# Products of the identity in TensorE's planned idle stretches, and conditioning products of 128 columns, in a two-block transformer kernel

## The chip, the cores and the metric

The kernel runs on one NeuronCore of a Trainium2 chip. The metric is the device time of one execution in microseconds (us); three runs of the kernel before gave 1361.81, 1362.93 and 1365.57. The engines are called PE (TensorE), DVE (VectorE), ACT (ScalarE), POOL (GpSimd) and SP (SyncE, which here only issues DMAs). Each executes its instructions in the order written, and waits on semaphores for the others.

## What is computed

The reference applies two transformer blocks to `x` of 16 x 256 x 256 (batch, length, channels), all in float32. The first block, conditioned on one vector per batch element, has three residual steps. The second, `L1`, is one cross attention whose norms are conditioned on other tensors.

```python
m = silu(mod) @ w_ada + b_ada                 # nine pieces of 256: shift, scale, gate x 3
h = _ln(x) * (1 + sc_msa) + sh_msa
x = x + _self_attn(h, ...) * g_msa            # 16 heads of 16, windows of 128, rolled by 64
h = _ln(x) * (1 + sc_mca) + sh_mca
x = x + _topk_cross_attn(h, context, ...) * g_mca   # softmax over the 16 largest of 256 scores
h = _ln(x) * (1 + sc_mlp) + sh_mlp
x = x + (silu(h @ w_a + b_a) * (h @ w_b + b_b) @ w_m2 + b_m2) * g_mlp    # hidden size 1024
...
ss = silu(c) @ W_ss + b_ss                    # L1: scale and shift of each norm
x = x + softmax(q k' / 4) v @ Wp + bp         # q from x, k and v from the context
```

## The kernel before

One function, `pixart_two_blocks`, treats the 16 batch elements one after another; the 256 positions of one lie as two tiles of 128 partitions. Every step is recorded with `op(...)` into a `Plan`: its engine, an estimated cost, the buffers it reads and writes, and a function that emits it. Each step also has a due time from a table (`DUE`, in thousandths of one batch element), found earlier and written into the file. `Plan.order` sorts all steps by due time; then it walks through them once with the estimated costs (`LAG`, `SWITCH`, and for DMAs `ISSUE`, `BEGIN`, `LAND`, `RATE`, `OPEN`) and keeps the time at which each engine is free. The walk does not change the order. What it decides is which of the free buffers of a kind a step takes: the one free first. `Plan.run` then emits the steps in that order, so that it is the order of every engine's queue. The kind `W` is the eight PSUM banks of 128 x 512; a bank goes back when its last reader's estimated end has passed.

The stages that the prediction speaks of, with their lines in the kernel before:

- **Conditioning** (`conditioned`, `ada_columns`, `gate_rows`). `condT` holds silu of the 16 vectors, turned to 128 channels x 2 x 16. `ada_columns` multiplies a 256 x 256 piece of a weight with it: four products (L703) with a 128 x 128 piece of the weight stationary and 16 columns of `condT` moving. DVE adds the bias (L709, L711). There are ten such pieces: six for the three norms of the first block and four for `L1`. `gate_rows` has `condT` stationary (L744); its rows go to DRAM and are loaded back for every batch element (`gate`, L377).
- **Self attention**: norm (DVE statistics L425 and L427, POOL L432 to L437 for `xn`), transposes against the identity (L449), shift and scale on ACT (L463), products with the weights (L475, and L511 for the values), scores (L780), their maxima on DVE (`maxima`, L588), which `lower` turns (L598) and sends with sixteen small DMAs into spare rows of the queries (L605), scores again the other way round (L788), exponentials (L612, ACT), the product with the values (L581), division (L538, L540 on DVE, `on` L541 on POOL), `oT` (L548), and the projection (L558), whose weights POOL has multiplied by the gate (`gw`, L404); ACT copies it out (L398) and POOL adds it to `x` (L399). `add_row` (L384) adds the gate's bias row to `x`.
- **Top-k attention**: scores (L827), then on DVE twice the eight largest (L846, L866) and their removal (L854, L871); exponentials on ACT (L859); POOL multiplies (`prT`, L875); transposes (L525), copies (L528), and L581.
- **Feed forward** (L888, L915) and the **last attention** (L932, L944).

From the second batch element on, these are interleaved: top-k of one element beside self attention of the next and feed forward and last attention of the one before. At the start there is only the first element, beside the loading of weights and the conditioning; at the end only the last one, which is treated in two halves.

```python
if o.eng == "PE" and o.mode != mode:
    t, mode = t + SWITCH[o.mode], o.mode
for p in o.after:
    t = max(t, p.end + (p.own if p.eng == o.eng else LAG.get(p.eng, 0.0)))
```

Of the kernel before, what the change touches and what calls it, by code (L numbers as in the profile page):

```python
# [163 lines left out]
SWITCH = {128: 0.18, 32: 0.2, 33: 0.12}  # L164
OWN = {"PE": 0.0, "DVE": 0.13, "ACT": 0.1, "POOL": 0.05}
LAG = {"PE": 0.22, "DVE": 0.14, "ACT": 0.18, "POOL": 0.1}
ISSUE, BEGIN, LAND, RATE, OPEN = 0.47, 0.9, 1.0, 320.0, 8


class Buf:  # L170
# [8 lines left out]


class Op:
    __slots__ = ("tag", "eng", "cost", "hold", "own", "kb", "emit", "due", "mode", "takes", "uses", "after", "start", "end", "n")


class Plan:
# [9 lines left out]
    def op(self, eng, cost, emit, r=(), w=(), also=(), mode=None, after=(), hold=None, own=None, kb=()):  # L195


        o = Op()
        o.hold, o.own, o.kb = cost if hold is None else hold, OWN.get(eng, 0.0) if own is None else own, kb
        o.eng, o.cost, o.emit, o.mode, o.n = eng, cost, emit, mode, len(self.ops)  # L200
        o.tag = self.tag
        o.after, o.takes, o.uses = {*after}, [], []
        for how, items in (("r", r), ("w", w), ("a", also)):
            for item in items:
                buf, key = item if isinstance(item, tuple) else (item, None)
                if buf.kind is not None and o not in buf.users:
                    buf.users.append(o)
                    o.uses.append(buf)
                if how == "a":
                    continue  # L210
                same = [k for k in {*buf.writers, *buf.readers} if key is None or k is None or k == key]
                for k in same:
                    if k in buf.writers:
                        o.after.add(buf.writers[k])
                    if how == "w":
                        o.after.update(buf.readers.get(k, ()))
        for how, items in (("r", r), ("w", w)):
            for item in items:
                buf, key = item if isinstance(item, tuple) else (item, None)
                if how == "r":  # L220
                    buf.readers.setdefault(key, []).append(o)
                else:
                    if key is None:
                        buf.writers, buf.readers = {}, {}
                    buf.writers[key] = o
                    buf.readers[key] = []
        o.after.discard(o)
        self.ops.append(o)
        return o

    def order(self):

        for o in self.ops:
            o.due = max([o.due, *(p.due for p in o.after)])
        done = sorted(self.ops, key=lambda o: (o.due, o.n))
        free, open_users, ends = {e: 0.0 for e in ("PE", "DVE", "ACT", "POOL", "SP")}, {}, {}  # L240
        slots = {k: [(0.0, n) for n in range(len(v))] for k, v in self.tiles.items()}
        mode, lanes, moved = None, [0.0] * OPEN, 0.0
        for o in done:
            t = free[o.eng]
# [4 lines that stand above are left out]
            for b in o.uses:  # L249
                if b.slot is None:  # L250
                    if not slots[b.kind]:
                        raise RuntimeError(f"no {b.kind} is free for {o.tag}, due {o.due}")
                    at, b.slot = slots[b.kind].pop(0)
                    t = max(t, at)
                    o.takes.append(b)
                    open_users[b], ends[b] = len(b.users), 0.0
            for b in o.uses:
                t = max([t, *(end for e, end in b.seen.items() if e != o.eng)])
            o.start = t
            for kb in o.kb:  # L260
                t = max(t, lanes.pop(0)) + ISSUE
                moved = max(t + BEGIN, moved) + kb / RATE
                lanes.append(moved + LAND)
            free[o.eng], o.end = (t, lanes[-1]) if o.kb else (t + o.hold, t + o.cost)
            for b in o.uses:
                if b.kind == "W":
                    b.seen[o.eng] = o.end + LAG[o.eng]
                ends[b] = max(ends[b], o.end + LAG.get(o.eng, 0.0))
                open_users[b] -= 1
                if not open_users[b]:  # L270
                    insort(slots[b.kind], (ends[b], b.slot))
        self.span = max(free.values())
        return done

    def run(self):
        for o in self.order():
            for b in o.takes:
                b.t = self.tiles[b.kind][b.slot]
            o.emit()


# [2 lines left out]
def pixart_two_blocks(ctx: ExitStack, tc: tile.TileContext, i: dict, out: bass.AP):  # L284
# [50 lines left out]
    for t in tiles["v"]:  # L335
        nc.gpsimd.memset(t[:, :, :, DH:NW], 1.0)
    plan = Plan(tiles)
    op = plan.op

    def rolled(ap, b):  # L340
# [288 lines left out]
        "L1_xcond_Wq", "L1_xcond_Wkv", "L1_xcond_Wp")}  # L629
    w_qkv, w_so, w_q, w_kv, w_co, w_m1, w_m2, w1_q, w1_kv, w1_p = weights.values()  # L630
    ada = {(how, g): fixed(f"ada_{how}_{g}", [P, NCC, B]) for how in ("shift", "scale") for g in (0, 1, 2, "q", "kv")}
    condT = fixed("condT", [P, NCC, B])

    last_row = fixed("last_row", [P, C])
    gates = [Buf(None, dram.tile([B, 2, C], F32, name=f"gates_{g}")) for g in range(3)]
# [37 lines left out]
    def conditioned():  # L673

        y, sy, w = Buf("h"), Buf("h"), Buf("W")
        op("SP", 0.0, lambda: nc.sync.dma_start(y.t[:B, :], i["cond_1024"]), w=[y], kb=(16,))
        op("ACT", 0.4, lambda: nc.scalar.activation(sy.t[:B, :], y.t[:B, :], AF.Tanh, scale=0.5), r=[y], w=[sy])

        def silu():
            nc.vector.scalar_tensor_tensor(sy.t[:B, :], sy.t[:B, :], 1.0, y.t[:B, :], ALU.add, ALU.mult)  # L680
            nc.vector.tensor_scalar(sy.t[:B, :], sy.t[:B, :], 0.5, None, ALU.mult)
        op("DVE", 0.8, silu, r=[y, sy], w=[sy])

        def emit():
            for c in range(NCC):
                nc.tensor.transpose(w.t[:, ts(c, B)], sy.t[:B, ts(c, P)], ident[:B, :B])
        op("PE", 0.3, emit, r=[sy], w=[w], mode=128)
        op("DVE", 0.2, lambda: nc.vector.tensor_copy(condT.t.rearrange("p c b -> p (c b)"), w.t[:, :NCC * B]), r=[w], w=[condT])

    def ada_piece(src):  # L690

# [4 lines left out]
    def ada_columns(dst, src, bias, chunk, plus_one):  # L696

        w, pm = ada_piece(src), Buf("W")

        def emit():  # L700
            for m in range(NCC):
                for c in range(NCC):
                    nc.tensor.matmul(pm.t[:, ts(m, B)], w.t[:, c, ts(m, P)], condT.t[:, c, :], start=c == 0, stop=c == NCC - 1)  # L703
        op("PE", 1.7, emit, r=[w, condT], w=[pm], mode=128)

        def out_of_it():
            for m in range(NCC):
                if plus_one:
                    nc.vector.tensor_scalar(dst.t[:, m, :], pm.t[:, ts(m, B)], col(bias, chunk + m), 1.0, ALU.add, ALU.add)  # L709
                else:  # L710
                    nc.vector.tensor_scalar(dst.t[:, m, :], pm.t[:, ts(m, B)], col(bias, chunk + m), None, ALU.add)  # L711
        op("DVE", 0.32, out_of_it, r=[pm, cols(bias)], w=[dst])


# [13 lines left out]
    def gate_rows(g, proj, value=None):  # L728

        rows = Buf("gate")  # L730
        off = (3 * g + 2) * C

        def emit():
            nc.sync.dma_start(rows.t[:B, 0, :], i["L0_xcond_b_ada"][off:off + C].partition_broadcast(B))
            nc.sync.dma_start(rows.t[:B, 1, :], i[proj].partition_broadcast(B))
        op("SP", 0.0, emit, w=[rows], kb=(16, 16))
        w, pg = ada_piece(i["L0_xcond_w_ada"][:, off:off + C]), Buf("W")
        if value:
            pv = value_bias(*value)
            op("DVE", 0.34, lambda: nc.vector.tensor_tensor(rows.t[:B, 1, :], pv.t[:B, :C], rows.t[:B, 1, :], ALU.add), r=[pv, rows], w=[rows])  # L740

        def product():
            for c in range(NCC):
                nc.tensor.matmul(pg.t[:B, :C], condT.t[:, c, :], w.t[:, c, :], start=c == 0, stop=c == NCC - 1)  # L744
        op("PE", 0.86, product, r=[w, condT], w=[pg], mode=128)

        def both():
            nc.vector.tensor_tensor(rows.t[:B, 0, :], pg.t[:B, :C], rows.t[:B, 0, :], ALU.add)
            nc.vector.tensor_tensor(rows.t[:B, 1, :], rows.t[:B, 0, :], rows.t[:B, 1, :], ALU.mult)
        op("DVE", 0.75, both, r=[pg, rows], w=[rows])  # L750
        op("SP", 0.0, lambda: nc.sync.dma_start(gates[g].t, rows.t[:B]), r=[rows], w=[gates[g]], kb=(32,))
# [344 lines left out]
```

## Time and profile before

| what | value |
|---|---|
| median of three runs | 1362.93 us (1361.81 to 1365.57) |
| the profiled execution | 1365.2 us |
| its span, first to last instruction | 1363.1 us |
| mean granted TensorE clock | 0.981 |
| PE busy | 1327.1 us, 97% of the span |
| DVE busy | 1216.9 us, 89% |
| ACT, POOL busy | 1014.4 us, 1026.4 us |
| chain that ended last | PE 87%, DVE 5% |

Times in the profile count from the start of the span. A row of the timeline gives start, duration, engine, line, operation, output and inputs, the size of the part of TensorE in use, the shapes and the number of merged instructions; in square brackets stands how long the engine had been idle before, and what ended that. A product in float32 appears as two records, a transpose as one. The granted clock is a record of its own, as a share of the full one.

### The profile page before, as it was taken

What the parts mean: (1) busy time and instruction counts of PE and PEld (TensorE: products, weight loads), DVE (VectorE), ACT (ScalarE), POOL (GpSimd) and SP (SyncE); (2) the same over time, 40 slices, a digit from 0 to 9 for tenths busy, and PEclk for the clock granted to TensorE, in tenths of its full rate; (3) what the DMA queues carried; (4) which work ended last, traced back from release to release, by engine and by line L of the source; (5) the groups of instructions that cost most, each with busy time, mean ns of one, the idle gap of its engine ahead of it and who ended that gap; (6) DMA issues with size and microseconds to landing.
All of it is one profiled execution on the core that took longest, in us unless ns stands there. A gap on an engine that the chain in (4) does not pass through costs nothing.

```text
span 1363.1 us, 38514 instructions
## 1 busy us (share of the span) xinstructions
PE 1327.1 (97%) x13464; PEld 1040.8 (76%) x13464; DVE 1216.9 (89%) x4357; ACT 1014.4 (74%) x2359; POOL 1026.4 (75%) x1552
## 2 busy tenths in 40 slices
PE   8699999999999999999999999999999999999996
PEld 6466787878778787877878787787878777787875
DVE  3699999999999999999999999999999999998734
ACT  4256778877777878777787878778787877877773
POOL 2456887878788787878878787787878787878752
PEclk9788999999999999999999999999999999999998
DMA  5412000101000010100001010001101000000000
GB/s 158 147 53 58 18 25 18 40 18 41 16 20 25 19 40 18 41 17 18 25 22 37 17 41 18 18 25 22 36 18 41 25 18 25 26 2 10 10 2 18
DMA packets 64161, 42.44 MB, mean 31 GB/s; under 512 B 37764, under 2 KB 56752, under 8 KB 63712
## 3 DMA queue, kind: packets, MB, share of 16 engines
q1 hardware_dynamic: 63967, 39.99, 10.9%
q8 instruction: 107, 1.75, 0.5%
q14 instruction: 87, 0.70, 0.2%
HBM read 35.14 MB, written 4.29 MB: 29 GB/s over the span
## 4 chain that ended last, share of the span: by engine, by line
PE 87%; DVE 5%; POOL 2%; DMA 2%; SPq 1%; issue 1%; ACT 1%; ACTq 0%; POOLq 0%; DVEq 0%
PE W L888 17%; PE W L475 11%; PE W L581 11%; PE W L525 8%; PE W L915 7%; PE W L511 6%; PE W L558 6%; PE W L944 5%; PE W L932 5%; PE W L827 5%; PE W L449 3%; PE W L788 3%; PE W L780 2%; DVE rest L854 1%; DVE rest L871 1%
## 5 line engine op out<-in xcount | busy, mean ns | idle before, releaser
L875 POOL TENSOR_TENSOR prT<-rest,prT 128x512 f32<-128x512 f32 x256 | 325.7, 1273 | 63.5 <-DVE rest L871 49.8
L859 ACT ACTIVATE prT<-W,ntop 128x256 f32<-128x256 f32 x512 | 216.8, 510 | 76.0 <-POOL ntop L848 64.3
L588 DVE TENSOR_REDUCE nm<-W 128x2 f32<-128x512 f32 (+1 forms) x384 | 236.9, 681 | 28.1 <-PE W L932 16.0
L888 PE MATMUL W<-xT,w_L_xcond_w_m 128*128 128x256 f32 (+1 forms) x1088 | 249.0, 375 | 1.5 <-ACT xT L463 1.5
L612 ACT ACTIVATE pTO<-W 128x512 f32<-128x512 f32 (+1 forms) x392 | 200.5, 613 | 62.0 <-PE W L944 37.6
L888 PEld LDWEIGHTS W<-xT,w_L_xcond_w_m 128*128 128x128 f32 x1088 | 189.1, 190 | 57.0 <-ACT pTO L612 10.9
L854 DVE MATCH_REPLACE8 rest<-top,W 128x256 f32<-128x256 f32 x512 | 208.2, 416 | 0.2 <-issue 0.2
L871 DVE MATCH_REPLACE8 rest<-top,rest 128x256 f32<-128x256 f32 x512 | 205.5, 409 | 0.0
L846 DVE MAX8 top<-W 128x8 f32<-128x256 f32 x512 | 187.0, 417 | 14.7 <-PE W L827 14.5
L866 DVE MAX8 top<-rest 128x8 f32<-128x256 f32 x512 | 187.3, 410 | 0.0
L525 PE MATMUL W<-ident,prT 128*128 128x128 f32 x1024 | 144.4, 279 | 11.1 <-POOL prT L875 11.1
L528 ACT ACTIVATE pTT<-W 128x512 f32<-128x512 f32 x256 | 148.4, 621 | 8.8 <-PE W L525 8.7
L541 POOL TENSOR_TENSOR on<-tr,rec 128x128 f32<-128x128 f32 (+1 forms) x162 | 71.0, 443 | 98.6 <-DVE rec L540 98.2
L525 PEld LDWEIGHTS W<-ident,prT 128*128 128x128 f32 x1024 | 120.3, 143 | 32.6 <-POOL prT L875 14.6
L905 POOL TENSOR_TENSOR mb<-ma,mb 128x256 f32<-128x256 f32 (+1 forms) x136 | 94.7, 697 | 62.7 <-ACT mb L903 50.6
L538 DVE STREAM_TRANSPOSE tr<-W 128x256 f32<-128x256 f32 (+1 forms) x162 | 79.2, 490 | 48.1 <-PE W L581 40.1
L915 PE MATMUL W<-w_L_xcond_w_m,h 128*128 128x256 f32 x512 | 113.8, 380 | 0.0
L581 PE MATMUL W<-pTO,v 128*32 128x128 f32 (+1 forms) x2112 | 108.1, 329 | 2.3 <-ACT pTO L612 2.0
L915 PEld LDWEIGHTS W<-w_L_xcond_w_m,h 128*128 128x128 f32 x512 | 95.9, 190 | 13.6 <-POOL prT L875 0.8
L908 POOL TENSOR_TENSOR h<-h,mb 128x256 f32<-128x256 f32 (+1 forms) x136 | 94.8, 697 | 8.3
L581 PEld LDWEIGHTS W<-pTO,v 128*32 128x32 f32 x2112 | 57.8, 111 | 42.6 <-ACT h L907 10.2
L903 ACT ACTIVATE mb<-W,half 128x256 f32<-128x256 f32 (+1 forms) x136 | 69.6, 513 | 9.7 <-PE W L888 8.4
(126 smaller groups left out, 2675.2 us busy)
## 6 DMA issues: line engine op xcount, KB each, us to landing
gate<-gates SPq DMA_DIRECT2D x48, 256.0 KB
q<-nmT SPq DMA_DIRECT2D x480, 1.0 KB
cx<-in_ctx_dram SPq DMA_DIRECT2D x19, 256.0 KB
cx<-in_ctx_dram SPq DMA_DIRECT2D x104, 32.0 KB
rest<-in_L_xcond_w_ada_dram SPq DMA_DIRECT2D x9, 256.0 KB
x<-in_x_dram SPq DMA_DIRECT2D x16, 128.0 KB
x<-in_x_dram SPq DMA_DIRECT2D x32, 64.0 KB
w_L_xcond_w_m<-in_L_xcond_w_m_dram SPq DMA_DIRECT2D x1, 2048.0 KB
```

The lines of the kernel that those rows point to most:

```text
L525: nc.tensor.transpose(w.t[:, ts(n, P)], flat[:, ts(n, P)], ident)
L581: nc.tensor.matmul(po.t[ds(NW * j, NW), ds(q0, nq)], v.t[:, kt, 8 * m + 2 * j + a, :], pT.t.rearrange("p n q -> p (n q)")[:, ds(part, nq)] ...
L588: op("DVE", 0.61, lambda j=j, s=s: nc.vector.tensor_reduce(nm.t[:, k, ds(j, groups, step=4)], s.t.rearrange("p (g k) -> p g k", g=groups), ...
L612: op("ACT", 0.24 + q * 0.0005, lambda s=s, pT=pT: nc.scalar.activation(pT.t.rearrange("p n q -> p (n q)")[:, :q], s.t[:, :q], AF.Exp), r=[ ...
L846: nc.vector.max(top.t[:, a, 0:8], s.t[:, ts(a, L)])
L854: nc.vector.match_replace(rest.t[:, a, :], top.t[:, a, 0:8], s.t[:, ts(a, L)], TAKEN)
L859: nc.scalar.activation(pr.t[:, a, :], s.t[:, ts(a, L)], AF.Exp, bias=ntop.t[:, a:a + 1])
L866: nc.vector.max(top.t[:, a, 8:16], rest.t[:, a, :])
L871: nc.vector.match_replace(rest.t[:, a, :], top.t[:, a, 8:16], rest.t[:, a, :], TAKEN)
L875: op("POOL", 1.25, lambda: nc.gpsimd.tensor_tensor(pr.t, rest.t, pr.t, ALU.mult), r=[rest, pr], w=[pr])
L888: nc.tensor.matmul(w.t[:, :q], w_m1.t[:, c, ds(n0, P)], xT.t[:, c, :q], start=c == 0, stop=c == NCC - 1)
L915: nc.tensor.matmul(pp.t[:, ts(k, C)], hs[f].t[:, ts(k, P)], w_m2.t[:, f, :], start=f == 0, stop=f == NHC - 1)
```

## The change

Three things are changed.

First, `order` marks stretches in which PE, by the estimates, sits idle for more than 1.0 us before a step. If a PSUM bank is free in time, the step gets a bank and a number `n`: as many products of an estimated 0.87 us as fit between the moment that both PE and the bank are free and 0.15 us before the step. The bank goes back to the free ones at the time of the step. `run` emits the `n` products ahead of the step: the identity times the identity repeated four times, 512 columns, into that bank. Nothing reads them.

Second, `condT` is widened from 16 to 128 columns, the rest of them zero, and `ada_columns` moves all 128; only the first 16 columns of the result are read. The product's estimated cost goes from 1.7 to 0.9. `gate_rows` still uses 16.

Third, two estimates for DMAs change: `ISSUE` from 0.47 to 0.53, and `LAND` from 1.0 to 0.4. The table of due times is the same.

```diff
-ISSUE, BEGIN, LAND, RATE, OPEN = 0.47, 0.9, 1.0, 320.0, 8
+IDLE, FILLER = 1.0, 0.87
+ISSUE, BEGIN, LAND, RATE, OPEN = 0.53, 0.9, 0.4, 320.0, 8
...
             o.start = t
+            if o.eng == "PE" and t - free["PE"] > IDLE and free["PE"]:
+                ok = slots["W"][:1]
+                n = int((t - max(free["PE"], ok[0][0]) - 0.15) / FILLER) if ok else 0
+                if n > 0:
+                    slot = slots["W"].pop(0)[1]
+                    insort(slots["W"], (t, slot))
+                    o.fill = self.tiles["W"][slot], n
...
                 b.t = self.tiles[b.kind][b.slot]
+            if o.fill:
+                self.filler(*o.fill)
             o.emit()
...
+    def filler(t, n):
+        for _ in range(n):
+            nc.tensor.matmul(t, ident, ident.unsqueeze(1).to_broadcast([P, 4, P]), start=True, stop=True)
+    plan.filler = filler
...
-    condT = fixed("condT", [P, NCC, B])
+    condT = fixed("condT", [P, NCC, P])
+    nc.vector.memset(condT.t, 0.0)
...
-                    nc.tensor.matmul(pm.t[:, ts(m, B)], w.t[:, c, ts(m, P)], condT.t[:, c, :], start=c == 0, stop=c == NCC - 1)
-        op("PE", 1.7, emit, r=[w, condT], w=[pm], mode=128)
+                    nc.tensor.matmul(pm.t[:, ts(m, P)], w.t[:, c, ts(m, P)], condT.t[:, c, :], start=c == 0, stop=c == NCC - 1)
+        op("PE", 0.9, emit, r=[w, condT], w=[pm], mode=128)
...
-                    nc.vector.tensor_scalar(dst.t[:, m, :], pm.t[:, ts(m, B)], col(bias, chunk + m), 1.0, ALU.add, ALU.add)
+                    nc.vector.tensor_scalar(dst.t[:, m, :], pm.t[:, ds(m * P, B)], col(bias, chunk + m), 1.0, ALU.add, ALU.add)
...
-                nc.tensor.matmul(pg.t[:B, :C], condT.t[:, c, :], w.t[:, c, :], start=c == 0, stop=c == NCC - 1)
+                nc.tensor.matmul(pg.t[:B, :C], condT.t[:, c, :B], w.t[:, c, :], start=c == 0, stop=c == NCC - 1)
```

## The prediction

> **What bounds the kernel now.** I read the page first. Over most of the span TensorE (PE) is full and VectorE (DVE) nearly so; only the first tenth and the last slice differ, and there the granted clock falls.
>
> ```profile
> PE   8699999999999999999999999999999999999996
> DVE  3699999999999999999999999999999999998734
> PEclk9788999999999999999999999999999999999998
> ```
>
> The second view is the table of stretches, cut where the clock changes (columns: stretch, length, busy time and instructions of PE, weight loads, DVE, ACT, POOL; clock, DMA share, GB/s).
>
> ```profile
> 15.36:32.43 17.07, 16.71 (x166) 13.70 (x164) 7.61 (x22) 11.71 (x25) 0.00 (x0) 1.00 0.33 102
> 32.43:46.08 13.65, 13.65 (x148) 10.35 (x147) 5.03 (x19) 3.93 (x8) 4.18 (x6) 0.50 0.63 191
> 46.08:63.15 17.07, 11.71 (x85) 8.02 (x84) 12.10 (x37) 4.48 (x10) 9.94 (x15) 1.00 0.35 125
> 63.15:80.21 17.06, 11.17 (x60) 7.50 (x60) 15.81 (x65) 7.21 (x16) 8.75 (x12) 0.50 0.21 64
> 80.21:100.70 20.49, 19.06 (x245) 14.69 (x244) 18.69 (x76) 13.99 (x31) 12.13 (x17) 1.00 0.11 33
> 100.70:110.94 10.24, 8.77 (x56) 5.97 (x56) 10.24 (x43) 6.57 (x15) 8.83 (x15) 0.50 0.15 44
> 134.68:1287.00 1152.32, 1150.87 (x11760) 905.88 (x11760) 1088.51 (x3914) 905.57 (x2099) 929.21 (x1379) 1.00 0.09 24
> ```
>
> The reader is to see three things. From 134.68 to 1287 PE idles 1.5 us in 1152: it is the bound, so what the start gains or loses reaches the end unchanged. The clock is halved from 32.43, 63.15 and 100.70 on, and again twice near the end; all steps are whole multiples of 3.41 us apart. The first 15.36 us are printed as clock 1.00, but eight records of L703 take 1.89 us there as in the halved stretch, against 1.06 at 29.44: they are slow too.
>
> The third view is the timeline of PE, with DVE's waits on it.
>
> ```profile
> 29.44 1.06 PE L703 MATMUL W<-condT,rest 128*128 128x16 f32 x8
> 36.20 2.09 PE L788 MATMUL W<-q,k 32*128 32x128 f32 x32
> 38.22 1.89 PE L703 MATMUL W<-condT,rest 128*128 128x16 f32 x8
> 68.24 1.11 PE L525 MATMUL W<-ident,prT 128*128 128x128 f32 x4 [8.86 <-POOL prT L875]
> 76.86 3.55 PE L511 MATMUL W<-w_L_xcond_w_kv,xT 128*128 128x256 f32 x8
> 81.94 1.17 PE L788 MATMUL W<-q,k 32*128 32x128 f32 x32
> 1317.18 1.06 PE L475 MATMUL W<-xT,w_L_xcond_Wq 128*128 128x128 f32 x8
> 1336.79 3.44 PE L932 MATMUL W<-k,q 32*128 32x256 f32 x32 [0.55 <-ACT q L497]
> ```
> ```profile
> 71.39 0.77 DVE L846 MAX8 top<-W 128x8 f32<-128x256 f32 x2 [1.08 <-PE W L827]
> 81.56 0.72 DVE L538 STREAM_TRANSPOSE tr<-W 128x512 f32<-128x512 f32 x1 [1.15 <-PE W L581]
> ```
>
> Up to about 59 us the chain of waits runs through PE, its exponentials and the small DMAs of `lower`; from 59.4 to 116 DVE is busy without a break but for those two waits on a slow PE and 0.65 us.
>
> **What the change does.** The instruction order of the changed kernel shows 26 fillers in 17 places: 18 up to about 133 us (nine places, one of them with ten, ahead of the transposes at 68.24) and 8 after 1290. SP, POOL and ACT keep their order, DVE gets one memset more, in its idle time before 2.92. PSUM banks change names, but from about 145 to 1287 every instruction waits for the same ones as before. So only start and tail move.
>
> **Prices.** A filler is one product of 512 columns, as much as four records of 256. L511's eight take 1.73 us in the chain at full clock and 3.35 at half, so a filler costs 0.87 or 1.7. Padding L703: the row at 1317.18 has its new shape (128*128, 128x128) and takes 1.06 us, what L703 takes now with 16 columns; the weight load sets it. I cost it at nothing; at half clock from 0 to +0.2 each.
>
> **Step 1, first products.** Today L475 starts at 12.09 (weights land at 11.96) and takes 5.30 us, against 3.62 at 23.99 with a full clock. The first filler stands before an L703 that idles 0.19, the second before L475, which idles 1.60. If the denser start has the clock up when L475 begins, it gains 1.7; if not, the two cold fillers (3.4 us) exceed the idle time and it ends up to 1.0 later. I take -0.7, between the ends.
>
> **Step 2, first self-attention, 31 to 59 us.** Filler three stands before L788, whose queries land at 31.39 - 0.7. PE gets there at 29.8, fills to 30.7, and the two halves of L788 end at 31.9 (now 32.25). If the clock holds: exponentials to 34.0 (2.06 as now), meanwhile L703 and filler four; L581 to 35.2; L788 at 1.17 in place of 2.09 to 36.4; L703 and filler five under the next exponentials; L581 to 39.6 (now 42.34). Here POOL comes in: it waits for the gate row (39.89 now, 39.2 then), and with `gw`, `add_row` and `on` ends at 42.3, so `oT` is there at 42.8, not 44.64. L558 then ends at 44.8 (now 48.14), and the latency chain L398, L399, statistics, `xn` keeps that shift. Filler six (behind L511, ends 50.3) is ready before `xn` (50.8). Filler seven costs 0.3 before L827, which ends at 56.45 in place of 59.42. **Top-k starts 2.95 us earlier**, of which 0.7 is step 1. What is late next is DVE: L740 needs a row that lands at 52.4 - 0.7, with its reductions it is ready at about 55.8, so there is little left behind it.
>
> **Step 3, the ten fillers.** They wait for the last L588 before L846, then need 8.7 us; the first transposed tile is 8.84 us after L846 starts. They fit with nothing to spare, and an overrun of up to 0.4 is hidden, since PE then has slack on DVE. With the clock up, L525 and L827 take 1.8 us in place of 3.2, DVE's wait of 1.08 goes, and L581 (cold L788 and L511 ahead of it) comes about 3 us earlier against DVE, so its wait of 1.15 goes too: **-2.2**. A third wait, 0.86 at 116.34 behind the stretch at 100.70, has no filler near it; I count 0, bound -0.86. The filler before L449 at 133.59 fills an idle 0.45 and 0.21 there: 0 to +0.3, taken as 0.
>
> **Step 4, tail.** Three fillers of 0.87 stand in idle times of 0.55 (L888 at 1291.13, L475 at 1334.96, L932 at 1336.79): +0.35 each, +1.05. The others fit into 0.93, 2.03 and 1.11, or run under exponentials. Against it, 32 records of L932 would take 2.3 in place of 3.44, worth 0.65 because four L588 follow; L944 and L558 behind 1346 save 1.7, of which 0.75 is left after the exponentials and a filler. Net **-0.4**, bounds -1.3 to +1.0.
>
> **Sum.** -2.95 - 2.2 - 0.4 = -5.5 us. Bounds: -8.3 with the best of steps 1, 3 and 4. The profiled execution took 1365.2 (span 1363.1), 2.3 above the median of 1362.93; so 1359.7 by its own time and 1357.4 from the median. Part of the 2.3 may be cold stretches that other executions lack, and these cannot be saved twice. I take the middle, **1358.5**.
>
> The Trainium skill (TensorE: Matmul & The Clock Gate, "What's actually happening") says that the clock is either half or full, judged in free-running windows of 3413 ns that don't start with the kernel. The trace agrees (0.50 and 1.00; 30.72 us from 32.43 to 63.15 are nine such windows). By that rule, where the cold stretches lie differs between executions.
>
> **Rivals.** *B: the fillers hold the clock less than hoped.* The first two run cold (+1.0 in place of -0.7), and after 66 us, where PE waits for DVE and nothing is filled, the clock falls again. Then top-k starts 1.25 us earlier and half of DVE's 1.08 goes, tail 0: -1.8, 1363.4 and 1361.1 by the two bases, **1362**. For it: 100.70 fell with PE 86% busy. Against it: L788 to L744 at full clock with fillers are dense.
>
> *C, slower: products of the identity do not hold the clock.* The place is the ten before the first transposes. Five run in the 5.1 us until it falls (one and a half windows), five cold: 4.4 + 8.5 = 12.9 against 8.84, +4.1, and DVE waits that much longer for L827. Fillers three to five, cold on a PE that today has no idle between 31.5 and 48, add 5.1; one and two 1.6; six and seven 0.6; the tail 1.0. Sum +12.4: **1375** (1377.6 and 1375.3, less what hides). It decides as soon as the ten start at half clock: 17 - 8.8 = 8.2 is above the whole gain. Against it: between 107.5 and 110.9, L581 and eight transposes against the same identity brought the clock back.
>
> The same page (Part 4, PE-mode transpose) says that transposes do not engage the full clock; by that rule, stretched to identity products, C would hold. The trace speaks against it at 110.94. No run here has yet shown the filler's own form.
>
> **Chances.** A measurement tells about 0.3% (4 us) from no change. Forecast 0.60: its own spread, 1354.5 to 1361, lies four parts in five below 1358.8, so 0.48 faster, 0.12 same. B 0.27: 0.02 faster, 0.25 same. C, with all that runs cold, 0.13 slower. That is 0.50, 0.37, 0.13. The range, 1354 to 1364, takes in the bounds of the sum and B; C is left out.
>
> **What would show it.** Right: no 0.50 clock between 20 and 66 us; L788 x32 in 1.17 near 35 us; the first L846 near 56.5; L525 right behind the tenth filler at 0.87 us each; DVE without the waits of 1.08 and 1.15; L449 of `xn` near 128.5 in place of 133.59; no halved window between 1336 and 1350. Wrong: fillers of 1.7 us, above all among the ten; top-k starting near 59 because the gate row or the row for L740 came last; a new fall of the clock between 66 and 100 that brings DVE's waits back.

## The result, and the profile after

The changed kernel takes a median of 1358.48 us (five runs, 1357.23 to 1358.97), the kernel before, beside it, 1362.93 (1361.81 to 1365.57). The ratio is 0.9963, 95% interval 0.9948 to 0.9977. The profiled execution took 1358.97 us with a span of 1356.9; against 1365.2 before, that is 6.2 us less, where the medians differ by 4.45. The profiled execution of before lies 2.27 above its median, that of the changed kernel 0.49. The first has a mean clock of 0.981, at the lower end of what the kernel before showed over all its runs here (0.981 to 0.991); the changed kernel had 0.994 to 0.998.

The page of the changed kernel, part 2 (the span in 40 slices, busy share and granted clock in tenths):

```profile
PE   8989999999999999999999999999999999999997
DVE  4799999999999999999999999999999999998834
PEclk9989999999999999999999999999999999999999
```

The 7 of the clock's second slice is a 9, of the two 8s behind it one is left, and the 8 of the last slice is gone; PE's second slice went from 6 to 9. The table of stretches shows the clock's falls themselves (same columns as in the prediction: length, busy time and instructions of PE, weight loads, DVE, ACT, POOL, then clock, DMA share, GB/s):

```profile
0.00:9.08 9.08, 5.09 (x17) 3.82 (x18) 4.52 (x25) 2.49 (x4) 4.72 (x16) 1.00 0.58 158
9.08:70.52 61.44, 57.33 (x494) 37.89 (x492) 36.51 (x125) 25.10 (x54) 21.19 (x33) 1.00 0.50 159
70.52:73.93 3.41, 3.20 (x15) 2.58 (x11) 3.41 (x16) 2.84 (x6) 2.73 (x3) 0.50 0.01 2
97.83:104.66 6.83, 5.96 (x47) 4.30 (x48) 6.83 (x31) 3.73 (x9) 6.40 (x10) 0.50 0.00 1
104.66:1356.00 1251.34, 1241.54 (x12697) 973.25 (x12696) 1142.33 (x4075) 965.39 (x2252) 976.78 (x1469) 1.00 0.09 24
```

Before, 47.8 us were halved (13.65, 17.07, 10.24 and twice 3.41); now 10.2 are, and none in the tail. The first row needs care: the clock is printed as 1.00 there, but its products run at half speed, as in the timeline of PE:

```profile
4.35 2.07 PE L721 MATMUL W<-condT,rest 128*128 128x128 f32 x8 [0.28 <-DVE condT L706]
7.44 1.93 PE L353 MATMUL W<-ident 128*128 128x512 f32 x2
9.20 1.05 PE L721 MATMUL W<-condT,rest 128*128 128x128 f32 x8
12.09 3.69 PE L492 MATMUL W<-xT,w_L_xcond_w_qkv 128*128 128x256 f32 x16 [0.54 <-DMA w_L_xcond_w_qkv<-in_L_xcond_w_qkv_dram]
56.15 8.85 PE L353 MATMUL W<-ident 128*128 128x512 f32 x20
1332.07 2.01 PE L950 MATMUL W<-k,q 32*128 32x256 f32 x32
```

L353 is the filler (two records each), and the lines of before that are named here are 17 or 18 further on. The first filler took 1.93, the padded L721 beside it 2.07 and then 1.05: full speed begins at 9.08 in this execution, and at 15.36 in the profiled one of before. L492 (L475 before) starts at 12.09 in both and takes 3.69 in place of 5.30. The ten fillers take 8.85, and L542 follows at 65.08 with no idle time. L950 (L932) takes 2.01 in place of 3.44.

From the first `MAX8` to 130 us, DVE's timeline has two waits on PE left:

```profile
56.24 0.76 DVE L864 MAX8 top<-W 128x8 f32<-128x256 f32 x2 [0.79 <-PE W L845]
110.74 0.76 DVE L864 MAX8 top<-W 128x8 f32<-128x256 f32 x2 [0.81 <-PE W L845]
```

The waits of 1.08 (at 71.39) and 1.15 (at 81.56) are gone. The second row is the third wait of before (0.86 at 116.34), still behind a halved stretch. The first was there before too, at the same instruction, and comes up again below:

```profile
59.40 0.76 DVE L846 MAX8 top<-W 128x8 f32<-128x256 f32 x2 [0.86 <-PE W L827]
```

It is easiest to compare kernels by three stages, each from one landmark to the next in the profiled execution: from the start to the first `MAX8` of top-k, from there to the first product of the feed forward (L888, now L906), and from there to the end of the span.

| kernel | to top-k | top-k to feed forward | to the end | profiled run, us | median, us |
|---|---|---|---|---|---|
| before | 59.40 | 76.28 | 1227.5 | 1365.2 | 1362.93 |
| changed | 56.24 | 73.86 | 1226.8 | 1358.97 | 1358.48 |
| e1 no fillers | 56.25 | 73.83 | 1227.7 | 1359.79 | 1359.79 |
| e2 16 columns | 57.07 | 74.06 | 1227.0 | 1360.12 | 1360.52 |
| e3 without ten | 56.02 | 73.82 | 1227.2 | 1359.03 | 1359.75 |
| e4 no tail | 56.07 | 73.58 | 1228.1 | 1360.17 | 1358.99 |
| f1 padding alone | 56.90 | 76.29 | 1226.7 | 1361.98 | 1360.24 |
| f2 all 16 | 59.16 | 76.40 | 1228.9 | 1366.47 | 1366.00 |
| f3 sixteen | 55.66 | 78.26 | 1226.9 | 1362.81 | 1363.03 |
| f4 one ahead of the first | 55.16 | 73.72 | 1226.0 | 1356.85 | 1357.12 |
| g1 two more at 95 | 55.55 | 74.57 | 1226.3 | 1358.44 | 1358.16 |
| g2 without the middle five | 54.60 | 74.09 | 1226.2 | 1356.94 | 1356.20 |
| h1 changed, again | 56.56 | 72.85 | 1226.8 | 1358.26 | 1359.03 |
| h2 is g2, again | 54.55 | 73.49 | 1226.3 | 1356.31 | 1356.59 |

The last column is told with intervals below. The kernel before ran beside each of the four groups of experiments (e, f, g, h), each group on another chip, with medians of 1363.30, 1362.86, 1363.43 and 1364.18.

### The profile page after: what moved, and what is told of

Read it like the earlier page. It is cut to its first block, busy times and chain, and to the rows that moved or that the text cites. A ratio compares the mean times of both kernels' runs of the same rounds, so it can differ in the third digit from the quotient of the medians.

```text
span 1356.9 us, 38607 instructions
## 1 busy us (share of the span) xinstructions
PE 1334.2 (98%) x13516; PEld 1037.8 (76%) x13516; DVE 1216.7 (90%) x4358; ACT 1015.7 (75%) x2359; POOL 1027.4 (76%) x1552
## 4 chain that ended last, share of the span: by engine, by line
PE 88%; DVE 5%; DMA 2%; ACT 2%; SPq 1%; issue 1%; POOL 1%; POOLq 0%; ACTq 0%; DVEq 0%
PE W L906 17%; PE W L492 12%; PE W L598 11%; PE W L933 8%; PE W L542 8%; PE W L528 6%; PE W L575 6%; PE W L962 5%; PE W L845 4%; PE W L950 4%; PE W L466 3%; PE W L806 2%; PE W L798 2%; DVE rest L872 1%; DVE nm L605 1%
## 5 line engine op out<-in xcount | busy, mean ns | idle before, releaser
L906 PE MATMUL W<-xT,w_L_xcond_w_m 128*128 128x256 f32 (+1 forms) x1088 | 248.7, 375 | 0.3 <-DVE nm L605 0.3
L906 PEld LDWEIGHTS W<-xT,w_L_xcond_w_m 128*128 128x128 f32 x1088 | 189.0, 190 | 56.6 <-ACT pTO L629 10.9
L542 PE MATMUL W<-ident,prT 128*128 128x128 f32 x1024 | 142.3, 276 | 3.2 <-POOL prT L893 2.6
L542 PEld LDWEIGHTS W<-ident,prT 128*128 128x128 f32 x1024 | 119.1, 142 | 24.0 <-POOL prT L893 6.2
L933 PEld LDWEIGHTS W<-w_L_xcond_w_m,h 128*128 128x128 f32 x512 | 95.9, 190 | 13.7 <-POOL prT L893 0.8
L598 PE MATMUL W<-pTO,v 128*32 128x128 f32 (+1 forms) x2112 | 105.5, 325 | 0.1
L598 PEld LDWEIGHTS W<-pTO,v 128*32 128x32 f32 x2112 | 56.3, 109 | 41.8 <-ACT h L925 9.4
```

Source lines behind the costliest of these rows:

```text
L542: nc.tensor.transpose(w.t[:, ts(n, P)], flat[:, ts(n, P)], ident)
L598: nc.tensor.matmul(po.t[ds(NW * j, NW), ds(q0, nq)], v.t[:, kt, 8 * m + 2 * j + a, :], pT.t.rearrange("p n q -> p (n q)")[:, ds(part, nq)] ...
L906: nc.tensor.matmul(w.t[:, :q], w_m1.t[:, c, ds(n0, P)], xT.t[:, c, :q], start=c == 0, stop=c == NCC - 1)
L933: nc.tensor.matmul(pp.t[:, ts(k, C)], hs[f].t[:, ts(k, P)], w_m2.t[:, f, :], start=f == 0, stop=f == NHC - 1)
```

## The experiments

The theory of the prediction is that the **fillers** keep the clock up. The rival that the trace suggests is that the **padding** does so: in the changed kernel L721 streams 128 columns through a stretch where L703 streamed 16. A third is that neither matters, and that the new DMA estimates and the other PSUM banks changed the waits. A fourth, for single groups of fillers: they cost as much as they bring.

### Fillers and padding taken apart

e1 has no fillers, but the padding and the estimates:

```diff
-                if n > 0:
+                if n > 99:
```

> The fillers are left out; the conditioning of 128 columns and the new DMA estimates stay. If the fillers hold the clock and so make the gain: back to 1362 to 1364 us, the clock halved again from about 32 us and about 63 us on, top-k's first L864 between 58 and 60 us. If the padding of the conditioning is what holds the clock: 1358 to 1360 us, full clock from about 15 to 60 us without a filler, the long idle time before the first transposes still followed by a halved clock.

Measured: 1359.79 (1358.78 to 1361.34), ratio 0.9973 (0.9961 to 0.9984). Top-k starts at 56.25, as with all fillers, but by two effects that cancel. Without the first two fillers the clock, up at 8.09, fell again from 11.50 to 14.91, L492 took 5.11, and the L721 that the changed kernel starts at 27.83 came at 29.20. What it lost there it won back behind that, where the other five fillers are missing; g2 below takes that apart. The stretch that was halved before stays at full clock:

```profile
32.43:46.08 13.65, 12.74 (x164) 8.50 (x163) 6.82 (x22) 4.23 (x9) 5.81 (x8) 1.00 0.60 179
```

e2 has the fillers, but moves 16 columns in `ada_columns`:

```diff
-                    nc.tensor.matmul(pm.t[:, ts(m, P)], w.t[:, c, ts(m, P)], condT.t[:, c, :], start=c == 0, stop=c == NCC - 1)
+                    nc.tensor.matmul(pm.t[:, ds(m * P, B)], w.t[:, c, ts(m, P)], condT.t[:, c, :B], start=c == 0, stop=c == NCC - 1)
```

> The fillers stay as they are; the conditioning products move 16 columns again. If the fillers carry the gain: 1358 to 1360 us, at most one more halved window between 30 and 45 us. If the padding matters as much: the clock halves between 30 and 46 us in spite of the fillers, top-k starts 1.5 to 3 us later than with the padding, 1360 to 1362 us.

Measured: 1360.52 (1359.37 to 1361.67), ratio 0.9980 (0.9972 to 0.9989); top-k at 57.07, clock full up to 71.73. That is the clock of its first forecast with the time of its second. Here, too, the L721 comes late, at 29.21, since full speed began at 13.71. So either part alone holds the clock from 32 to 46 us, and either alone brings half to three quarters of the whole gain (2.0 and 2.7 thousandths of 3.7). f1 is the kernel before with the padding and its lower cost estimate only; the DMA estimates are as they were (in part; ... stands for lines left out):

```diff
-    condT = fixed("condT", [P, NCC, B])
+    condT = fixed("condT", [P, NCC, P])
+    nc.vector.memset(condT.t, 0.0)
...
-                    nc.tensor.matmul(pm.t[:, ts(m, B)], w.t[:, c, ts(m, P)], condT.t[:, c, :], start=c == 0, stop=c == NCC - 1)
-        op("PE", 1.7, emit, r=[w, condT], w=[pm], mode=128)
+                    nc.tensor.matmul(pm.t[:, ts(m, P)], w.t[:, c, ts(m, P)], condT.t[:, c, :], start=c == 0, stop=c == NCC - 1)
+        op("PE", 0.9, emit, r=[w, condT], w=[pm], mode=128)
```

> The kernel before with the conditioning of 128 columns alone; no fillers, the old DMA estimates. If the padding by itself keeps the clock up through the first self attention: as without fillers, 1359.5 to 1360.5 us, no halved clock between 30 and 55 us, top-k's first L846 at 56.0 to 56.5 us. If the new estimates (other PSUM banks) had a share in that: 1361.5 to 1363.5 us.

Measured: 1360.24 (1358.21 to 1362.10), ratio 0.9979 (0.9970 to 0.9988); top-k at 56.90. Its interval and that of e1 overlap, so the DMA estimates are not needed for the gain.

f2 keeps everything of the changed kernel, also the number of fillers, their banks and waits, but fillers and `ada_columns` move only 16 columns (the edit of e2, and this):

```diff
-            nc.tensor.matmul(t, ident, ident.unsqueeze(1).to_broadcast([P, 4, P]), start=True, stop=True)
+            nc.tensor.matmul(t[:, :B], ident, ident[:, :B], start=True, stop=True)
```

> The changed kernel with conditioning products of 16 columns and fillers of 16 columns: as many products at the same places with the same weight loads, banks and waits, but hardly any columns. If the clock goes by moving columns: as before the change, 1362 to 1364.5 us, halved from about 32 to 46 us and after 60 us. If it goes by TensorE being occupied, or if waits and banks made the gain: 1358.5 to 1360.5 us.

Measured: 1366.00 (1362.24 to 1367.47), ratio 1.0019 (1.0009 to 1.0029). That is slower than the kernel before; in the profiled execution by the last stage (1228.9 against 1227.5). The stretch from 32.43 is halved again, with PE busy for all of it:

```profile
32.43:46.08 13.65, 13.65 (x151) 10.72 (x150) 5.03 (x19) 3.85 (x8) 4.16 (x6) 0.50 0.62 188
```

In its timeline of PE the scores (L806, 2.09 in place of 1.17) and L721 are back at half speed, and the short fillers run among them:

```profile
38.13 1.89 PE L721 MATMUL W<-condT,rest 128*128 128x16 f32 x8
59.08 2.40 PE L353 MATMUL W<-ident 128*128 128x16 f32 x20
```

This settles the third theory: with the same instructions, banks and waits, but few columns, the clock falls at 32.46, 63.18 and 100.73, where before had 32.43, 63.15 and 100.70. What the clock goes by is how much is streamed, not that PE has an instruction at work. The 3.41 us ahead of the fall at 32.46 show it best; here is that stretch of f2, and below it the same stage in f1, where the clock stayed up:

```profile
29.05:32.46 3.41, 3.28 (x48) 2.80 (x47) 1.45 (x10) 2.78 (x7) 0.00 (x0) 1.00 0.06 11
30.18:33.60 3.42, 3.17 (x48) 2.73 (x46) 1.26 (x9) 2.88 (x6) 0.00 (x0) 1.00 0.05 11
```

PE is busy for 3.28 us in f2 and for 3.17 in f1; what differs is above all the columns of L721 (L704 in f1). It is no accident of one profile: the mean clock over the eleven runs is 0.981 to 0.989 for f2 and 0.986 to 0.992 for f1, 0.989 to 0.991 over seven runs of e1, and 0.994 to 0.997 over twelve of e2.

### The ten and the tail

e3 leaves out only the group of ten (`n` is 10 there), e4 only the fillers of the tail (`t` is the estimated time):

```diff
-                if n > 0:
+                if 0 < n < 5:
```

> The ten fillers before the first transposes are left out; all others stay. By the prediction's step 3 they are worth 2.2 us: top-k starts near 56.3 us as with them, the clock halves near 60 us, DVE waits for L845 and L598 again (about 1.1 and 1.2 us), 1360.7 us. If DVE covers a cold PE there: 1358.5 us, no such waits.

```diff
-                if n > 0:
+                if n > 0 and t < 200:
```

> The eight fillers of the last 75 us are left out; those of the start stay. The prediction's step 4 gives them 0.4 us: 1358.9 us. The trace of the changed kernel, whose shift grew by 1.5 us in the tail, says 1360 us, with two halved windows between 1330 and 1346 us again. If they only cost time: 1357.5 us.

Measured for e3: 1359.75 (1359.03 to 1361.15), ratio 0.9971 (0.9961 to 0.9981). Without the ten the clock is halved from 58.93 to 69.17, and DVE waits for L845 a little longer than in the changed kernel (2.1 against 1.6 in all), but the stage takes 73.82 against 73.86. DVE's waits of e3 from 55 to 128 us (columns: total, times, longest):

```profile
DVE top L864 <- PE W L845: 2.1, 3, 1.1
```

And those of f1, which has no fillers either:

```profile
DVE top L847 <- PE W L828: 1.9, 2, 1.1
DVE tr L538 <- PE W L581: 1.2, 1, 1.2
```

The difference is the length of the halved stretch. In f1 it runs from 60.90 to 77.97, in f2 and before to 80.2, and all three have the wait on L581 and a stage of 76.3 or 76.4. In e1 and e3 it ends at 69.5 and 69.2, L581 (L598 there) runs at full clock, and the stage takes 73.8. So the ten are worth about 2.4 us in an execution whose cold stretch would be the long one, and nothing where it would be the short one. Which it is should go with where the 3.41 us steps lie in that execution; with one profile of each kernel that is not shown. On the medians, 0.7 to 1.3 us (1359.75 against 1358.48 and 1359.03), with overlapping intervals.

Measured for e4: 1358.99 (1357.59 to 1361.87), ratio 0.9968 (0.9955 to 0.9980), not told apart from the changed kernel. Its profiled execution has halved steps at 1330.92 and 1341.16, and the last stage takes 1228.1 in place of 1226.8, so there the tail's fillers are worth 1.3; the medians give 0 to 0.5.

### What a filler costs where it does not fit

f3 puts sixteen in place of the ten:

```diff
-                    o.fill = self.tiles["W"][slot], n
+                    o.fill = self.tiles["W"][slot], n if n < 5 else 16
```

> The changed kernel with sixteen fillers in place of the ten before the first transposes (16 columns of conditioning are not meant here; nothing else changes). Six more at 0.87 us delay L542 and L845 by 5.2 us. DVE has about 1 us to spare before it needs L845: 1358.5 + 4 = 1362 to 1363 us, and DVE waits about 4 us for L845 near 70 us. If PE catches up later all the same: 1358 to 1359.5 us.

Measured: 1363.03 (1362.32 to 1364.32), ratio 1.0003 (0.9994 to 1.0011). Timeline of PE, then DVE's waits:

```profile
55.58 14.00 PE L353 MATMUL W<-ident 128*128 128x512 f32 x32
69.42 0.60 PE L542 MATMUL W<-ident,prT 128*128 128x128 f32 x4
```
```profile
DVE top L864 <- PE W L845: 5.6, 3, 4.6
```

Sixteen at 0.87 each end 13.84 after the first began; DVE then waits 4.6 for the scores behind them, and the median is 4.3 us (mean of its two groups of runs) above that of the changed kernel. The whole gain of the change is gone with six fillers too many. It also shows the identity product holding the clock by itself: over these 14 us PE does nothing else, and the clock is 1.00.

f4 adds one filler ahead of the very first product, where PE idles 3.7 us; g1 adds to that two ahead of the transposes near 95 us, where the clock still falls (`turn` counts PE's steps; in part):

```diff
+MORE = {0: 1}
...
+            if o.eng == "PE":
+                turn += 1
+            if o.eng == "PE" and turn in MORE and slots["W"]:
+                slot = slots["W"].pop(0)[1]
+                insort(slots["W"], (t, slot))
+                o.fill = self.tiles["W"][slot], MORE[turn]
+            elif o.eng == "PE" and t - free["PE"] > IDLE and free["PE"]:
...
```

> The changed kernel with one more filler ahead of the first product, where PE idles for its first 3.7 us. If an earlier rise of the clock shortens the first products: between 0 and 0.7 us less by how the windows lie, 1357.5 to 1358.5 us; the first L492 waits for its weights at 12 us either way, so nothing where the clock was up by then. If the cold filler delays the first product: +0.2.

In g1 the first line is `MORE = {0: 1, 62: 2}`.

> The changed kernel with one filler ahead of the first product and two more where TensorE idles 1.75 us for L542 near 95 us. Where the clock was full there, DVE's wait for L845 near 110 us was 0.20 us, otherwise 0.81. If the clock fell for want of columns: no halved clock between 96 and 104 us, that wait down to 0.2 us, 0.6 us less than with the first filler alone: 1356.5 us. If the idle time is too short in one of the windows all the same, or DVE covers it: 1357.1 us.

Measured for f4: 1357.12 (1356.82 to 1357.84), ratio 0.9957 (0.9943 to 0.9971). The clock is up at 7.76, and top-k starts at 55.16. But the L721 of 27.83 is not earlier (28.03); the 1.08 at top-k are those of a row from DRAM that DVE waits for (L758, here L765, at 50.50 in place of 51.58). So the earlier clock is not what is seen to help. The interval overlaps that of the changed kernel, and f4 was not run beside it. For g1: 1358.16 (1357.49 to 1358.44), ratio 0.9963 (0.9950 to 0.9975), and this missed its aim, as the timeline of PE shows:

```profile
95.38 3.46 PE L360 MATMUL W<-ident 128*128 128x512 f32 x4 [2.65 <-ACT prT L884]
```

The two fillers waited 2.65 us themselves, for the bank that ACT was still reading, and then ran cold (1.7 each), since the clock had fallen at 95.74 in the meantime. The transposes L549 behind them came at 98.64, and DVE waited 1.6 us for POOL's `prT`, which f4 does not show.

g2 is the changed kernel without its five single fillers between 28 and 55 us; the padding stays:

```diff
-            if o.eng == "PE" and t - free["PE"] > IDLE and free["PE"]:
+            if o.eng == "PE":
+                turn += 1
+            if o.eng == "PE" and t - free["PE"] > IDLE and free["PE"] and turn not in (20, 22, 25, 33, 36):
```

> The changed kernel without the five single fillers between 28 and 55 us; the first two, the ten and the tail's stay, and the conditioning of 128 columns. If the padding alone holds the clock there: no halved clock before 60 us, top-k starts at 56.0 to 56.5 us, 1358.0 to 1359.0 us. If those fillers are needed: the clock halves between 30 and 46 us, top-k starts at 57 us or later, 1359.5 us or more.

Measured: 1356.20 (1355.81 to 1356.95), ratio 0.9950 (0.9936 to 0.9963). It was then run again beside the changed kernel:

> The changed kernel as it is, beside the next one on the same chip. Both theories: about 1358.5 us, between 1357.2 and 1359.0 as before.

> The changed kernel without its five single fillers between 28 and 55 us, beside the changed kernel on the same chip. Theory one (with the padding those five hold a clock that is held anyway, and each delays scores that PE could have started earlier): about 1356.2 us, 2 us under the changed kernel of this call, with the two ranges apart. Theory two (the earlier difference of 2.3 us came from comparing two calls): the two medians lie within 1 us.

Measured: h1 1359.03 (1358.26 to 1359.33), ratio 0.9964 (0.9952 to 0.9976); h2 1356.59 (1356.06 to 1357.69), ratio 0.9948 (0.9936 to 0.9961). On one chip, the kernel without the five is 2.4 us faster, with ranges apart; it is the fastest version found. What the five do is seen in the timeline of PE, first of the changed kernel, then of g2 (its lines are two further on):

```profile
28.83 1.02 PE L353 MATMUL W<-ident 128*128 128x512 f32 x2
29.78 1.17 PE L806 MATMUL W<-q,k 32*128 32x128 f32 x32
...
54.02 1.12 PE L353 MATMUL W<-ident 128*128 128x512 f32 x2 [0.51 <-DVE nm L605]
55.08 1.14 PE L845 MATMUL W<-k,q 32*128 32x512 f32 x8
```
```profile
28.75 0.73 PE L808 MATMUL W<-q,k 32*128 32x128 f32 x16
29.71 0.73 PE L808 MATMUL W<-q,k 32*128 32x128 f32 x16 [0.23 <-DMA q<-nmT]
...
53.02 1.14 PE L847 MATMUL W<-k,q 32*128 32x512 f32 x8 [0.56 <-ACT q L505]
```

In g2 half of the first scores start at 28.75, because half of the queries are there; a filler of 1.02 makes both halves wait. By 49 us `xn` is turned 1.06 later in the changed kernel (49.40 against 48.34). Then filler seven waits for a bank that DVE is reading, and L845 starts 2.06 later than in g2. But most of that is not what top-k waits for, as DVE's timeline shows, again first the changed kernel, then g2:

```profile
51.58 0.41 DVE L758 TENSOR_TENSOR gate<-W,gate 16x256 f32<-16x256 f32 x1 [3.39 <-PE W L798]
```
```profile
50.81 0.41 DVE L760 TENSOR_TENSOR gate<-W,gate 16x256 f32<-16x256 f32 x1 [3.67 <-DMA gate<-in_L_xcond_b_co_dram]
54.60 0.73 DVE L866 MAX8 top<-W 128x8 f32<-128x256 f32 x2
```

DVE waits for the row that L758 adds (L740 before). The profile of the changed kernel names L798, that of h1, the same kernel, the row. From there to the first `MAX8` it takes 4.66 us in the changed kernel and 3.79 in g2, where the scores lie ready: the difference is the 0.87 of one filler, the seventh. It is the same in all profiled executions that have a full clock there: 4.66 to 4.90 in the eight with filler seven (the changed kernel, e2 to e4, f3, f4, g1, h1), 3.79 to 3.90 in the four without (e1, f1, g2, h2). The other 0.77 of the 1.64 at top-k is the row itself, 51.58 against 50.81. In the changed kernel and those that keep its padding and the five (e3, e4, f3, f4, g1, h1) it came between 50.50 and 51.90, in g2 and h2 at 50.81 and 50.65. So filler seven is shown to cost 0.87; whether fillers three to six delay the row, or what else makes up the rest of the 2.4, is not shown. The mean clock is the same with and without the five (0.994 to 0.998 and 0.994 to 0.997): with the padding in place, they hold nothing.

## Why the prediction was right, and where it was not

The time was right, 1358.5 against 1358.48, and so was the source of the gain: the start and the tail run at full clock, and what the start gains reaches the end. That the two figures agree to 0.02 is luck. Over the profiled executions the sum was -5.5 and came out as -6.2, from parts that were off by -0.9, +0.7, -0.2, +0.8 and -1.1; and the middle between the two bases (1359.7 and 1357.4) was taken because the 2.3 us over the median might be cold stretches that others lack, which the mean clocks bear out; that half was the right share, nothing showed. What keeps the clock up was not as predicted either.

- **Step 1**: -0.7 predicted; the L703 at 29.44 comes at 27.83, -1.6. It is near the bound of 1.7 for a clock that is up when L475 begins. The step spoke of the fillers alone. In the nine profiled executions that have the padding and the first two fillers, full speed began between 7.5 and 10.4 us, and that row came at 27.55 to 28.04. In the five that lack one or leave out the columns (before, e1, e2, f1, f2) it came at 29.20 to 29.87, and full speed began, or in e1 came back, between 13.7 and 16.5. So the start took both parts together, as far as one profiled execution of each tells.
- **Step 2**: -2.25 predicted behind step 1; measured 3.16 - 1.61 = -1.55. The step that failed is "I cost it at nothing" for the padding, with the gain given to fillers three to five. The price of the padding was nearly right (1.05 to 1.16 for the padded eight records against 1.06), but what it does to the clock was left out: e1, f1 and g2 keep the clock without those fillers. Mis-sized was "filler seven costs 0.3": it costs 0.87. The row for L740, which the step put at 51.7, came at 51.58, and in all twelve executions with a full clock there DVE waits ahead of L758 for 2.7 to 4.8 us, in nine of them for the row by the profile. The row and filler seven set the start of top-k.
- **Step 3**: -2.2 predicted, 73.86 - 76.28 = -2.4 measured, both waits gone, the ten at 0.885 each with L542 right behind. But e3 has the same -2.4 without them. The missing piece is that, without the ten, the stage came out at two lengths, by when its cold stretch ends; before's profile showed the longer one, and an execution with the shorter needs no ten (72.85 in h1, where no step is halved up to 96 us, is the best that was seen). The third wait stayed at 0.81, as counted.
- **Middle**: nothing predicted. By 1276 us, 0.8 of 5.6 had been given back in small idle times, such as 0.32 ahead of L906 at 377; why was not tried.
- **Tail**: -0.4 predicted, about -1.5 measured (the shift goes from -4.7 to -6.2), a little beyond the bound of -1.3. The three fillers in idle times of 0.55 cost 0.15, 0.15 and 0.23, not 0.35 each: ahead of L906 at 1286.58, for one, 0.70 lie between PE's other products. The rest is L950 at 2.01 and L575 at 1.99 (before 3.44 and 2.67).
- **Rival B** is refuted for the changed kernel (no clock below 1.00 between 9.08 and 70.52, and only the first filler cold), but near what e1, e2 and f1 give, 1359.8 to 1360.5 where it said 1362. Its fall after 66 us came, at 70.52, for one step only.
- **Rival C** is refuted: the identity holds the clock (f3). The Trainium skill (TensorE: Matmul & The Clock Gate, Part 4, PE-mode transpose) says that transposes don't engage the full clock; stretched to these products it would have given C, and the runs go against that stretch. The filler is an ordinary product, so they leave the sentence itself open. The Trainium skill (same page, "What's actually happening") says that the chip counts no instructions, but watches how active PE is; f2 against the changed kernel agrees (as many instructions, 1366.00 against 1358.48). f2 adds that a PE which the profile shows busy for 13.65 of 13.65 us can be left at half clock, in a stretch where L721 moves 16 columns.
- "26 fillers in 17 places" should have been 16 places.

It stays open why most executions of one kernel fall on a few phases of the clock's steps (seven of eleven of f2 have a mean clock of 0.981), and how large a share of a step must be streamed.

## What to carry to other kernels

When the granted clock falls while PE's row says busy, look at how many columns its products move: a product of 16 columns that is bound by its weight load can be padded to 128 at little cost in time (here at most 0.1 us in 1.06), and that alone kept the clock up from 16.5 to 60.9 us (f1, ratio 0.9979). Fill idle time only where it is long, known, and has no other remedy: a filler is late work for what stands behind it, it waits for its own PSUM bank, the kernel without five needless ones was 2.4 us faster here, and six beyond the gap cost 4.3. Before a gain is credited to one of two parts, run each alone: here each alone brought half or more of the gain, because either kept the stretch from 32 to 46 us warm, while a full clock by 12 us was seen only with both.

## What the runs showed of the hardware

- The clock follows the streaming, not the time that PE is busy (busy 3.28 of 3.41 us ahead of a fall in f2, 3.17 of 3.42 in f1 with no fall). L721's eight records take 1.06 us with 16 columns and 1.05 to 1.16 with 128, but with 128 about four fifths of that is streaming and with 16 a tenth (an estimate from the filler: 512 columns in 0.87 us, four products of 128 columns then also 0.87).
- The printed clock is 1.00 ahead of the first step up, although products run at half speed there (2.07 against 1.05 for the same row, at 4.35 and 9.20).
- Where the clock was held, the spread was narrower too: the kernel before took 1360.7 to 1366.6 over its 68 runs beside the experiments, f2 1362.2 to 1367.5 over eleven, g2 and h2 together 1355.8 to 1357.7 over eleven.
